# Aggregation of a graph attention layer as seven products of quarters, on numerators normalized in front of it

## The chip, the cores and the metric

The kernel runs on one core of one Trainium2 chip. The metric is device microseconds of one execution; lower is better. Engines are named as in the profile: PE is TensorE's matmul, PEld its weight load, DVE is VectorE, ACT is ScalarE, POOL is GpSimd, SP is SyncE, whose queue issues the DMAs.

## The reference

Two layers follow each other on `x` of 64 graphs with 256 nodes and 512 features in float32; one adjacency matrix `adj` (256 x 256) holds for all graphs. Layer 0 is a graph attention whose weights come from a sum of two logits of the nodes, layer 1 an attention with 8 heads. Cut to what matters:

```python
# layer 0
h = jnp.maximum(_layernorm(x, axis=-1), 0.0)
Wh = jnp.einsum('bnd,de->bne', h, W)
e_src = jnp.einsum('bnd,d->bn', Wh, a_src)
e_dst = jnp.einsum('bnd,d->bn', Wh, a_dst)
logits = e_src[:, :, None] + e_dst[:, None, :]
logits = jnp.where(logits >= 0, logits, 0.2 * logits)
logits = jnp.where(mask, -jnp.inf, logits)          # mask = adj == 0
attn = jax.nn.softmax(logits, axis=-1)
x = x + jnp.einsum('bnm,bmd->bnd', attn, Wh)
# layer 1
h = jnp.maximum(_layernorm(x, axis=-1), 0.0)
q, k, v = (split_heads(h @ Wn.T + bn) for n in 'qkv')
attn = softmax(where(mask, -inf, q k^T / 8))
x = x + (attn v, heads joined) @ Wo.T + bo
```

## The kernel before, in words

A group is one graph: two tiles of 128 nodes by 512 features. There are G = 64 groups. The stages of a group are Python generators; each step of one writes a few instructions. An order that is written out by hand (`first_half` and `second_half`, one entry for each step, with a number that says how many groups ahead of the loop's group the step works) interleaves the steps of up to six groups. One pass through the two lists is a cycle of the steady state. Within an engine, instructions run in the order written; across engines they are tied by semaphores.

TensorE's products in a cycle, by letter: O is the output projection of layer 1 (two groups back), K the projection to q and k, V to v, W layer 0's transform by `W`, U0 and US layer 0's aggregation, X1 the transposition of the normalized rows for layer 1, E0 the weights of layer 0, A the attention's scores, masks and products with v. O, W, V and K are each written as **seven products of quarters**: a product of a 2 x 2 block matrix with another takes seven block products instead of eight if sums of blocks are formed first and sums of products afterwards. `combine` (L163) forms four sums of quarters of the left side on GpSimd, `combine_w` those of the weights once at the start, `products` (L170) writes the seven products, each into its own bank of PSUM, and `add_up` (L189, the adds L192 to L203) adds the products on VectorE. For product 0 ScalarE copies instead (L762 for v).

A product in float32 gives two records in the trace for each matmul instruction, each with its weight load.

Layer 0 in a group:

- `normalize0` (N0, D0): ScalarE forms means and squares (L457, L463), GpSimd the inverse deviations (L474 to L476), ScalarE h (L504), VectorE four sums of products with two weight rows (L511), which are the nodes' logits `es` and `ed`; the unused product goes into the scratch tile `junk`.
- `weights0` (E0, three steps): TensorE transposes `es` into `pe` (L525); ScalarE takes two exponentials (L532, L533) into `e1` and `e2`. Then VectorE takes their maximum (L537), and GpSimd multiplies with the mask (`em`, L540) and adds the two tiles (`esum`, L542). Last, TensorE sums over nodes (`ps`, L556) and VectorE takes the reciprocal (`rb`, L558, L559).
- `aggregate0` (U0 twice, then US): `pu` = the numerators `em` times `h`, transposed, as 8 matmul instructions with 256 columns in two banks (L572); VectorE multiplies each bank with the reciprocals into `uT` (L579). In US `combine` forms the sums `us` for the transform.
- `transform0` (W): seven products with `W`, added to the rows of x (L643).

In layer 1, `normalize1` (N1) writes `xn` (L671), `transpose1` (X1) transposes it (`pt`, L692) and writes `hT` (L693), then `combine` forms `hs`. `scale` (AS) multiplies the heads' results `aT` with the reciprocals of their sums (L878), which SP's queue has spread by eight DMAs into `rb` of the attention; `combine` then forms `as`. `bias_rows` (BO) adds the bias to the rows on GpSimd (L871). `attention` masks the exponentials (L793), adds them (L795), and takes the reciprocals of the sums (L828).

All banks of PSUM (8) are one pool; a product takes the bank that came free first, so it waits for the reader of an earlier product:

```python
def bank(shape, name):
    return ps_mm.tile(shape, F32, tag="mm", name=name)
```

Around U0 the written order of a cycle is `... V, V, V, A, N0, N1, U0, V, AS, U0, X1, V, X1, V, X1` and then, in the next pass, `(load), O, D0, K, AS_OLD, O, K, O, E0, K, E0, ...`. So VectorE has, in this order: the adds of V, a mask of A, the multiplication of the first U0, the adds of V, the scaling of aT, the multiplication of the second U0, two adds of V, the add of O, the four L511. ScalarE has h, xn and then hT.

Of the kernel before, what the change touches and what calls it, by code (L numbers as in the profile page):

```python
# [9 lines left out]
F32 = mybir.dt.float32  # L10
I32 = mybir.dt.int32
AF = mybir.ActivationFunctionType
ALU = mybir.AluOpType
# [3 lines left out]
P = 128  # L17
# [7 lines left out]
END = object()  # L25
# [3 lines left out]
def kernel(  # L29
# [26 lines left out]
    nc = tc.nc  # L56
    B, N, D = x.shape
    NC = N // P
    DC = D // P
# [4 lines left out]
    HD = D // 2  # L64
# [67 lines left out]
    def bounded():  # L132
# [9 lines left out]
        B11, B21, B22, T1, T2, T3, T4N = range(7)  # L142
# [115 lines left out]
        def node_weights():  # L258

            wa_c = weights.tile([P, 2, DC], F32, tag="wa_c", name="wa_c")  # L260
            a_rows = [bank([P, D], f"pa_{j}") for j in range(2)]
            for j in range(2):
                nc.tensor.matmul(a_rows[j], ones[0:1, :], a_in[:, j, :], start=True, stop=True)
            pas = [bank([P, D], f"pwa_{j}") for j in range(2)]
            for c in range(DC):
                if c == DC // 2:
                    busy(4)
                for j in range(2):
                    junk = work.tile([P, D], F32, tag="junk", name=f"junk_a_{j}_{c}")
                    nc.vector.scalar_tensor_tensor(  # L270
                        junk, a_rows[j], 1.0, w_c[c // 2][:, c % 2, :], op0=ALU.mult, op1=ALU.mult,
                        accum_out=wa_c[:, j, c : c + 1],
                    )
                    nc.tensor.transpose(
                        pas[j][:, c * P : (c + 1) * P], wa_c[:, j, c : c + 1].to_broadcast([P, P]),
                        ident,
                    )
                    if c >= DC // 2:
                        busy(2)
            return pas  # L280
# [36 lines left out]

        def output_bias():

            terms = work.tile([P, 2, HD], F32, tag="junk", name="terms")  # L320
            for c in range(DC):

                rows = wo_sb[:, B11 : T3 + 1 : T3 - B11] if c < 2 else wo_sb[:, B21 : B22 + 1]
                part, bv_c = rows[:, :, c % 2, :], cols["bv"][:, c : c + 1]
                if c == 0:
                    nc.vector.tensor_scalar(terms, part, bv_c, None, op0=ALU.mult)
                else:
                    nc.vector.scalar_tensor_tensor(
                        terms, part, bv_c, terms, op0=ALU.mult, op1=ALU.add
                    )  # L330
            yield
            pb = bank([P, D], "pbias")
            nc.tensor.matmul(pb, ones, terms.rearrange("p j e -> p (j e)"), start=True, stop=True)
            nc.vector.tensor_add(bo_b, pb, bo_b)
            yield
# [23 lines left out]
        def constants():  # L359
# [46 lines left out]
                yield  # L406
            sq = weights.tile([P, 4], F32, tag="sq", name="sq")
            for j, col in enumerate((cols["bq"], cols["bk"])):
                junk = work.tile([P, DC], F32, tag="junk", name=f"junk_c_{j}")
                nc.vector.scalar_tensor_tensor(  # L410
                    junk, col, 1.0, col, op0=ALU.mult, op1=ALU.mult, accum_out=sq[:, j : j + 1]
                )
# [7 lines left out]
            )  # L420
            yield
            for j in range(2):
                junk = work.tile([P, D], F32, tag="junk", name=f"junk_w_{j}")
                nc.vector.scalar_tensor_tensor(
                    junk, wa[j], 1.0, wa[j], op0=ALU.mult, op1=ALU.mult, accum_out=sq[:, 2 + j : 3 + j]
                )
                yield
# [53 lines left out]
        def normalize0(g):  # L481

            xt = xts[g]
            h = big.tile([P, NT, D], F32, tag="h", name=f"h_{g}", bufs=2)
            es = small.tile([P, NT], F32, tag="es", name=f"es_{g}")
            ed = small.tile([P, NT], F32, tag="ed", name=f"ed_{g}")
            if g == 1:

                mv, rstd = norm_stats(xt, f"0_{g}", small)
                nmr = small.tile([P, NT], F32, tag="nmr", name=f"nmr0_{g}")  # L490
                nc.gpsimd.tensor_scalar(nmr, mv[:, :, 0], -1.0, 0.0, op0=ALU.mult, op1=ALU.add)
                nc.gpsimd.tensor_tensor(nmr, nmr, rstd, op=ALU.mult)
                yield
            else:
                stats = Stats(xt, h, f"0_{g}")
                for t in range(NT):
                    stats.mean(t)
                yield
                for t in range(NT):
                    stats.squares(t)  # L500
                nmr, rstd = stats.close()
                yield
            for t in range(NT):
                nc.scalar.activation(  # L504
                    h[:, t, :], xt[:, t, :], AF.Relu, bias=nmr[:, t : t + 1], scale=rstd[:, t : t + 1]
                )
            yield
            for t in range(NT):
                for dst, a in ((es, 0), (ed, 1)):
                    junk = work.tile([P, D], F32, tag="junk", name=f"junk_{g}_{t}")  # L510
                    nc.vector.scalar_tensor_tensor(  # L511
                        junk, (wa if g else pas)[a], 1.0, h[:, t, :], op0=ALU.mult, op1=ALU.mult,
                        accum_out=dst[:, t : t + 1],
                    )
            nodes[g] = h, es, ed
            yield

        def weights0(g):
# [41 lines left out]
            edges[g].append(rs)  # L560
            yield

        def aggregate0(g):

            h = nodes.pop(g)[0]
            em = edges[g][0]
            uT = big.tile([P, DC, TOK], F32, tag="uT", name=f"uT_{g}")
            for dp in range(0, DC, 2):
                pu = bank([P, 2, N], f"pu_{g}_{dp}")
                for d in range(2):  # L570
                    for m in range(NC):
                        nc.tensor.matmul(  # L572
                            pu[:, d, :],
                            h[:, m, (dp + d) * P : (dp + d + 1) * P],
                            em[:, m, :],
                            start=(m == 0),
                            stop=(m == NC - 1),
                        )
                nc.vector.tensor_mul(  # L579
                    uT[:, dp : dp + 2, :], pu, edges[g][1].unsqueeze(1).to_broadcast([P, 2, N])  # L580
                )
                yield

            def a(t, j):
                return uT[:, 2 * j : 2 * j + 2, t * P : (t + 1) * P]

            del edges[g]
            sums0[g] = a, four_sums("us", g)
            combine(a, sums0[g][1])
            yield  # L590
# [366 lines left out]
        def aside(n=1):  # L957
            for _ in range(n):
                next(side, END)

        K, V, W, O = (project_qk, 0), (project_v, 0), (transform0, 1), (output, -2)
        N0, D0, E0, U0 = (normalize0, 3), (normalize0, 2), (weights0, 2), (aggregate0, 2)
        US, N1, X1 = (aggregate0, 1), (normalize1, 1), (transpose1, 1)
        A, A_OLD, BO = (attention, 0), (attention, -1), (bias_rows, 0)
        AS, AS_OLD = (scale, -1), (scale, -2)
        first_half = [
            (load, 3), O, D0, K, AS_OLD, O, K, O, E0, K, E0, O, K, O, US, A_OLD, K, O, K, BO, O, K, E0,
        ]
        second_half = [
            A_OLD, A, A, W, N0, W, W, V, N0, W, W, W, N1, W, N1, A, V, V, V, A, N0, N1, U0, V, AS,  # L970
            U0, X1, V, X1, V, X1,
        ]

# [23 lines left out]
        for i in range(G + 1):  # L997
            if i == G - 2:
                load_wo()
            todo = first_half + second_half  # L1000
            if i == 0:
                todo = first + [A, A, W, N0, E0] + second_half[5:19] + second_half[20:]
            elif i >= G - 1:
                todo = end if i == G else last
            for n, (stage, ahead) in enumerate(todo):
                if i == 0 and n in (5, 10):
                    next(bias)
                if i == 0 and n == 12:
                    combine_w(wv_sb)
                if i == 0 and n == len(first) + 1:  # L1010
                    combine_w(wq_sb)
                    prepare_biases()
                if i == 0 and n == len(first) + 18:
                    combine_w(wk_sb)
                if i == 1 and n == 4:
                    step(attention, 0)
                if i == 1 and n == 9:
                    combine_w(wo_sb)
                if i == 1 and n == 13:
                    step(bias_rows, 0)  # L1020
                step(stage, i + ahead)
                if i and n % 4 == 1:
                    aside()
# [209 lines left out]
```

## Time and profile before

| what | value |
|---|---|
| median of 3 runs | 2868.86 us (2867.56 to 2870.16) |
| the profiled execution | 2867.64 us, of which the span of the instructions is 2865.9 us |
| granted TensorE clock | 1.0 |
| busy: PE, DVE, ACT, POOL | 2848.8, 2343.6, 1235.0, 1214.5 us |
| a cycle of the steady state (one group) | 44.08 us |
| aggregation pu<-em,h (L572) | 1008 records, 238.1 us busy |
| multiplication uT<-pu,rb (L579) | 126 instructions, 682 ns mean |
| GpSimd's sums of quarters (L165 to L168) | 733 to 1162 ns each, by what runs beside them |

A line of a timeline reads: start in us from the span's start, length in us, engine, line of the kernel, operation, written tile <- read tiles, shape, number of instructions merged; in brackets, idle time of that engine before it and what ended it. Where several are merged, the length goes from the first start to the last end, and the ends of matmuls are modelled, so paces are read from starts.

### The profile page before, as it was taken

Reading aid. Unit: us, or ns where it says so; the run is one execution under the profiler, and the core shown is the slowest. Engines: PE = TensorE matmul, PEld = TensorE weight load, DVE = VectorE, ACT = ScalarE, POOL = GpSimd, SP = SyncE. Lnnn points to the kernel's source line nnn. Section 1 sums busy time; section 2 is a strip of 40 time slices with the busy share of each in tenths; the row PEclk is TensorE's granted clock in tenths of the full one; section 3 lists DMA queues with packets and bytes.
Section 4 is the critical chain, followed back from the end, with each engine's and each line's share of the span. In section 5 each row is a group of like instructions: output and inputs, shape, how many; then the busy total and the mean of one; then the engine's idle time right before and its main releaser. Section 6 shows DMA issues by size and latency. Waiting matters only on the chain. (4 is left out here: it accounts for less than half of the span.)

```text
span 2865.9 us, 50571 instructions
## 1 busy us (share of the span) xinstructions
PE 2848.8 (99%) x19584; PEld 2461.1 (86%) x19584; DVE 2343.6 (82%) x3641; ACT 1235.0 (43%) x2984; POOL 1214.5 (42%) x1406
## 2 busy tenths in 40 slices
PE   9999999999999999999999999999999999999998
PEld 6888888888888888888888888888888888888886
DVE  7888888888888888888888888888888888888875
ACT  5444444443543444435434444354344443443432
POOL 3444534435445344354453443544534435445331
PEclk9999999999999999999999999999999999999999
DMA  4122122221221222212212222122122221221221
GB/s 133 23 38 38 34 41 33 36 45 31 38 38 34 41 33 35 45 31 38 38 33 41 33 35 45 30 38 39 32 41 33 36 45 31 38 40 32 34 41 28
DMA packets 82810, 110.82 MB, mean 39 GB/s; under 512 B 11524, under 2 KB 48644, under 8 KB 82566
## 3 DMA queue, kind: packets, MB, share of 16 engines
q1 hardware_dynamic: 82470, 107.53, 23.5%
q8 instruction: 157, 2.57, 0.3%
q14 instruction: 87, 0.71, 0.1%
q0 software_dynamic: 96, 0.01, 0.0%
HBM read 41.43 MB, written 33.55 MB: 26 GB/s over the span
## 5 line engine op out<-in xcount | busy, mean ns | idle before, releaser
L643 DVE TENSOR_TENSOR x<-po,x 128x1024 f32<-128x1024 f32 x875 | 594.4, 686 | 209.9 <-PE po L207 203.0
L474 POOL TENSOR_SCALAR ve<-ssq 128x2 f32<-128x2 f32 x127 | 25.0, 197 | 1072.3 <-ACT h L463 827.7
L793 DVE TENSOR_TENSOR ex<-ex,maskT 128x512 f32<-128x512 f32 x512 | 361.1, 747 | 0.0
L788 ACT ACTIVATE ex<-psc 128x512 f32<-128x512 f32 x512 | 257.7, 627 | 90.2 <-PE psc L780 90.2
L813 ACT COPY aT<-pav 128x512 f32<-128x512 f32 x128 | 74.9, 585 | 498.5 <-PE pav L805 467.4
L216 PEld LDWEIGHTS pqk<-hs,wq_sb 128*128 128x128 f32 x2016 | 264.4, 192 | 12.9
L216 PE MATMUL pqk<-hs,wk_sb 128*128 128x128 f32 x2016 | 266.3, 275 | 0.0
L216 PE MATMUL pqk<-hs,wq_sb 128*128 128x128 f32 x2016 | 265.8, 275 | 0.0
L511 DVE SCALAR_TENSOR_TENSOR junk<-wa,h 128x512 f32<-128x512 f32 x252 | 255.1, 1012 | 12.5 <-ACT h L504 1.1
L207 PE MATMUL pv<-wv_sb,hs 128*128 128x256 f32 x1024 | 262.8, 379 | 0.6 <-DVE v L194 0.5
L207 PE MATMUL po<-wo_sb,as 128*128 128x256 f32 x992 | 255.2, 380 | 0.0
L207 PE MATMUL po<-w_sb,us 128*128 128x256 f32 x1008 | 248.5, 379 | 0.0
L216 PEld LDWEIGHTS pqk<-hs,wk_sb 128*128 128x128 f32 x2016 | 245.4, 192 | 0.0
L780 PE MATMUL psc<-qk 64*128 64x256 f32 x2048 | 239.0, 383 | 1.0 <-DVE rc L828 1.0
L572 PE MATMUL pu<-em,h 128*128 128x256 f32 x1008 | 238.1, 379 | 0.0
L805 PE MATMUL pav<-ex,v 128*64 128x256 f32 x2048 | 235.4, 382 | 0.0
L780 PEld LDWEIGHTS psc<-qk 64*128 64x128 f32 x2048 | 193.1, 187 | 47.6 <-issue 25.0
L740 ACT ACTIVATE p<-pqk,bias 128x128 f32<-128x128 f32 x252 | 71.8, 367 | 346.5 <-PE pqk L216 346.5
L828 DVE RECIPROCAL rc<-psm 128x256 f32<-128x256 f32 x64 | 112.4, 1756 | 133.0 <-PE psm L820 133.0
L871 POOL TENSOR_TENSOR x<-x,bo_b 128x512 f32<-128x512 f32 x128 | 218.2, 1723 | 0.0
L805 PEld LDWEIGHTS pav<-ex,v 128*64 128x64 f32 x2048 | 141.4, 137 | 85.6 <-DVE x L643 19.9
L207 PEld LDWEIGHTS po<-w_sb,us 128*128 128x128 f32 x1008 | 191.4, 190 | 26.2 <-DVE x L643 0.2
(188 smaller groups left out, 5880.9 us busy)
## 6 DMA issues: line engine op xcount, KB each, us to landing
x<-in_x_dram SPq DMA_DIRECT2D x64, 512.0 KB, 5.6
out_dram<-x SPq DMA_DIRECT2D x128, 256.0 KB, 2.0
rb<-rc SPq DMA_DIRECT2D x496, 64.0 KB, 4.9
wq_sb<-in_L_gnn_Wq_dram SPq DMA_DIRECT2D x4, 256.0 KB, 8.5
wk_sb<-in_L_gnn_Wk_dram SPq DMA_DIRECT2D x4, 256.0 KB, 6.6
w_sb<-in_L_gnn_W_dram SPq DMA_DIRECT2D x4, 256.0 KB, 6.6
wv_sb<-in_L_gnn_Wv_dram SPq DMA_DIRECT2D x4, 256.0 KB, 6.6
wo_sb<-in_L_gnn_Wo_dram SPq DMA_DIRECT2D x4, 256.0 KB, 6.0
```

The costliest lines, as they stand in the source:

```text
L207: nc.tensor.matmul(dst[:, 0:HD], left[:, c, :], wt[:, slot, c, :], start=c == 0, stop=c == 1)
L216: nc.tensor.matmul(dst[:, at : at + P], wt[:, slot, c, e * P : (e + 1) * P], left[:, c, :], start=c == 0, stop=c == 1,)
L511: nc.vector.scalar_tensor_tensor(junk, (wa if g else pas)[a], 1.0, h[:, t, :], op0=ALU.mult, op1=ALU.mult, accum_out=dst[:, t : t + 1],)
L572: nc.tensor.matmul(pu[:, d, :], h[:, m, (dp + d) * P : (dp + d + 1) * P], em[:, m, :], start=(m == 0), stop=(m == NC - 1),)
L643: nc.vector.tensor_add(dst, src, dst)
L780: nc.tensor.matmul(psc[r][:, m, :], qk[rows, 2 + e % 2, m * P : (m + 1) * P], qk[rows, e % 2, :], start=True, stop=True,)
L788: nc.scalar.activation(ex[:, r, :, :], psc[r], AF.Exp, scale=SCALE)
L793: nc.vector.tensor_mul(ex[:, r, :, :], ex[:, r, :, :], maskT)
L805: nc.tensor.matmul(pav[r * DH : (r + 1) * DH, i, :], v[j][:, m, at : at + DH], pair[i][:, r, m, :], start=(m == 0), stop=(m == NC - 1),)
L813: nc.scalar.copy(aT[j], pav)
L828: nc.vector.reciprocal(rc, psm)
L871: nc.gpsimd.tensor_tensor(part, part, bo_b, op=ALU.add)
```

## The change

For groups 3 to 63 the aggregation is written as seven products of quarters, like the projections. A new stage `quarters0` (Q0), one step early in the second half, forms on GpSimd the four sums of quarters of `h` (`hq`), multiplies the numerators `em` in place with the reciprocals (two instructions), and forms four differences of quarters of `em` (`eq`). `aggregate0` then writes seven products, each two matmul instructions of 128 columns into a bank of its own, four in its first step and three in its second; ScalarE copies product 0 into `uT`, VectorE adds up the others with seven adds. The multiplication with the reciprocals behind the products is gone. Groups 1 and 2 keep the old form (group 0 has its own path).

Two steps of E0 move in the written order: the one with the transpositions and exponentials is now behind the third K of the cycle instead of the second, the one with the maximum and the mask behind the fourth K instead of the third.

To make room in SBUF, the scratch tiles `junk` use the buffer of `e2`, and `terms` that of `rb`. New lines of the kernel after are 58 higher from `aggregate0`'s end on.

```diff
-                    junk = work.tile([P, D], F32, tag="junk", name=f"junk_{g}_{t}")
+                    junk = work.tile([P, D], F32, tag="e2", name=f"junk_{g}_{t}")
...
+        PLAIN = 3
+
+        def quarters0(g):
+
+            if g >= PLAIN:
+                h = nodes[g][0]
+                em, rb = edges[g]
+
+                def a(i, k):
+                    return h[:, k, i * HD : (i + 1) * HD]
+
+                s = big.tile([P, 4, HD], F32, tag="hq", name=f"hq_{g}")
+                combine(a, s)
+                for m in range(NC):
+                    nc.gpsimd.tensor_tensor(em[:, m, :], em[:, m, :], rb, op=ALU.mult)
+
+                def quarter(k, j):
+                    return em[:, k, j * P : (j + 1) * P]
+
+                t = work.tile([P, 4, P], F32, tag="eq", name=f"eq_{g}")
+                for to, x, y in (
+                    (0, quarter(0, 1), quarter(0, 0)), (1, quarter(1, 1), t[:, 0]),
+                    (2, quarter(1, 1), quarter(0, 1)), (3, quarter(1, 0), t[:, 1]),
+                ):
+                    nc.gpsimd.tensor_tensor(t[:, to], x, y, op=ALU.subtract)
+                right = {B11: quarter(0, 0), B21: quarter(1, 0), B22: quarter(1, 1)}
+                for to, slot in enumerate((T1, T2, T3, T4N)):
+                    right[slot] = t[:, to]
+                nodes[g] = h, (a, s, right)
+            yield
+
         def aggregate0(g):
 
-            h = nodes.pop(g)[0]
+            h, parts = nodes.pop(g)[0:2]
             em = edges[g][0]
             uT = big.tile([P, DC, TOK], F32, tag="uT", name=f"uT_{g}")
-            for dp in range(0, DC, 2):
+            if g >= PLAIN:
+                left, s, right = parts
+                s2 = work.tile([P, 4, P], F32, tag="s2", name=f"s2u_{g}")
+
+                def product(dst, left, slot):
+                    for e in range(2):
+                        nc.tensor.matmul(
+                            dst[:, e * P : (e + 1) * P], left[:, e * P : (e + 1) * P], right[slot],
+                            start=True, stop=True,
+                        )
+
+                def dst(i, j):
+                    return uT[:, 2 * i : 2 * i + 2, j * P : (j + 1) * P]
+
+                def read(n, ps):
+                    ps = ps[:, 0:HD].rearrange("p (e n) -> p e n", e=2)
+                    if n == 0:
+                        nc.scalar.copy(dst(0, 0), ps)
+                    add_up(n, ps, dst, s2[:, 0:2, :])
+
+                step_of = products(left, s, f"pu_{g}", product, read)
+                for n in range(7):
+                    next(step_of)
+                    if n in (3, 6):
+                        yield
+                assert next(step_of, END) is END
+            for dp in range(0, DC, 2) if g < PLAIN else ():
...
+        Q0 = (quarters0, 2)
...
         first_half = [
-            (load, 3), O, D0, K, AS_OLD, O, K, O, E0, K, E0, O, K, O, US, A_OLD, K, O, K, BO, O, K, E0,
+            (load, 3), O, D0, K, AS_OLD, O, K, O, K, E0, O, K, E0, O, US, A_OLD, K, O, K, BO, O, K, E0,
         ]
         second_half = [
-            A_OLD, A, A, W, N0, W, W, V, N0, W, W, W, N1, W, N1, A, V, V, V, A, N0, N1, U0, V, AS,
+            A_OLD, A, Q0, A, W, N0, W, W, V, N0, W, W, W, N1, W, N1, A, V, V, V, A, N0, N1, U0, V, AS,
             U0, X1, V, X1, V, X1,
         ]
```

More of the change, by code (lines that the diff above doesn't have):

```diff
@@ L268, in node_weights @@
                 for j in range(2):
-                    junk = work.tile([P, D], F32, tag="junk", name=f"junk_a_{j}_{c}")
+                    junk = work.tile([P, D], F32, tag="e2", name=f"junk_a_{j}_{c}")
                     nc.vector.scalar_tensor_tensor(
@@ L318, in output_bias @@
         def output_bias():
-            terms = work.tile([P, 2, HD], F32, tag="junk", name="terms")
+            terms = work.tile([P, 2, HD], F32, tag="rb", name="terms")
             for c in range(DC):
@@ L408, in constants @@
             for j, col in enumerate((cols["bq"], cols["bk"])):
-                junk = work.tile([P, DC], F32, tag="junk", name=f"junk_c_{j}")
+                junk = work.tile([P, DC], F32, tag="e2", name=f"junk_c_{j}")
                 nc.vector.scalar_tensor_tensor(
@@ L422, in constants @@
             for j in range(2):
-                junk = work.tile([P, D], F32, tag="junk", name=f"junk_w_{j}")
+                junk = work.tile([P, D], F32, tag="e2", name=f"junk_w_{j}")
                 nc.vector.scalar_tensor_tensor(
@@ L1001, in bounded @@
             if i == 0:
-                todo = first + [A, A, W, N0, E0] + second_half[5:19] + second_half[20:]
+                todo = first + [A, A, W, N0, E0] + second_half[6:20] + second_half[21:]
             elif i >= G - 1:
```

## The prediction

> **What bounds the kernel now.** I read the busy shares first, then one steady cycle in a window, then the timeline of TensorE, and last the waits. The busy shares (engine, busy us, share of the span, instructions):
>
> ```profile
> PE 2848.8 (99%) x19584; PEld 2461.1 (86%) x19584; DVE 2343.6 (82%) x3641; ACT 1235.0 (43%) x2984; POOL 1214.5 (42%) x1406
> ```
>
> TensorE is busy for the whole span, but ends of matmuls are modelled, so a share of 99% alone proves little. The timeline tells it by the starts. The aggregations of one group begin at 1390.08 us, those of the next at 1434.16 us: a cycle is 44.08 us. In the window of that cycle (length, busy us of PE, PEld, DVE, ACT, POOL) all other engines have room:
>
> ```profile
> 1390.08:1434.16 44.08, 44.08 (x305) 38.40 (x304) 36.44 (x57) 19.09 (x47) 19.26 (x22) 1.00 0.24 37
> ```
>
> The TensorE timeline around the change (start, length, engine, line, tiles, count):
>
> ```profile
> 1390.08 1.89 PE L572 MATMUL pu<-em,h 128*128 128x256 f32 x8
> 1391.81 1.03 PE L207 MATMUL pv<-wv_sb,hs 128*128 128x256 f32 x4
> 1392.67 1.89 PE L572 MATMUL pu<-em,h 128*128 128x256 f32 x8
> 1394.40 0.60 PE L692 MATMUL pt<-ident,xn 128*128 128x128 f32 x4
> 1394.84 1.03 PE L207 MATMUL pv<-wv_sb,hT 128*128 128x256 f32 x4
> 1395.70 0.60 PE L692 MATMUL pt<-ident,xn 128*128 128x128 f32 x4
> 1396.14 1.03 PE L207 MATMUL pv<-wv_sb,hs 128*128 128x256 f32 x4
> 1397.01 1.03 PE L207 MATMUL po<-wo_sb,aT 128*128 128x256 f32 x4
> 1397.87 1.05 PE L216 MATMUL pqk<-hT,wq_sb 128*128 128x128 f32 x8
> 1398.76 1.06 PE L216 MATMUL pqk<-hT,wk_sb 128*128 128x128 f32 x8
> ```
>
> The reader is to see that each start is the start before it plus the records' own pace: nothing waits. A record of 256 columns goes by 0.216 us (1.73 us for 8), one of 128 columns by 0.111 us (0.89 us for 8). So the time is the sum of TensorE's records, and a change pays if it takes records away and lets nothing make TensorE wait. The list of waits agrees: VectorE, ScalarE and GpSimd wait for TensorE, and TensorE's own waits are small.
>
> **What the Trainium skill says.** "TensorE: Matmul & The Clock Gate", section "Wait — 56ns, not 53.3ns?", has a small fixed cost for each matmul beside its columns. The trace agrees in kind: two records of 128 columns take 0.222 us, one of 256 takes 0.216. "SBUF — State Buffer", section "Who interferes with whom", says that a VectorE instruction with two SBUF inputs contends with a GpSimd instruction that reads SBUF. The trace agrees: the add at L199, beside GpSimd's adds of the bias, takes 1710 ns, its twin at L198 692. "VectorE: DVE Perf Modes", section "The DRAIN you can't avoid", lets no VectorE instruction start before the one ahead has emptied the pipe, with a semaphore costing nothing more. The trace differs: adds of 0.41 us start 0.33 apart when independent, 0.51 apart when the second needs the first (L192 to L194, 1389.97 to 1390.48). I take the trace.
>
> **The change part by part.** 61 of the 64 groups get it (groups 3 to 63).
>
> TensorE. Removed for a group: 8 products of 256 columns, 16 records, 16 x 0.216 = 3.46 us. Added: 7 products of two matmuls of 128 columns, 28 records. No row shows them; the nearest is L216, same shape and a weight load for each, 0.111 us: 28 x 0.111 = 3.11 us. Lower bound: the pace of the transpositions, 0.109 (0.44 us for 4), 3.05 us; upper: busy time by record with the pipeline's tail, 266.3 / 2016 = 0.132, 3.70 us. I take 0.111. Gain 0.34 us of a group, 61 x 0.34 = 20.7 us.
>
> VectorE. Removed: two multiplications at L579, 0.68 us each. Added: seven adds of 128x256 out of PSUM at 0.41 us, as for v at L192 to L203. Busy +1.5 us, 37.9 of 43.74 us: not the bound, but late in one place. ScalarE: one copy of 128x256 more, 0.37 us as at L762. It stands behind the normalization of xn (L671):
>
> ```profile
> 1390.22 1.50 ACT L504 ACTIVATE h<-x,nmr,rstd 128x512 f32<-128x512 f32 x2
> 1391.92 1.52 ACT L671 ACTIVATE xn<-x,nmr,rstd 128x512 f32<-128x512 f32 x2 [0.20 <-POOL nmr L476]
> ```
>
> That is the critical place; I follow it in the clock of this cycle. TensorE would be done with products 0 to 3 at 1391.86, a product of v at 1392.73, products 4 to 6 at 1394.06, and then go on 0.34 us earlier than in the timeline above: first transposition 1394.06, v 1394.50, second transposition 1395.36, v 1395.80, output product 1396.67. Weight loads want their data 0.1 to 0.2 us before. ScalarE's copy of product 0 runs from 1393.35 to 1393.72; its bank is the one that the first transposition takes: slack 0.2. VectorE's first add needs the copy: 1393.77 to 1394.18; its bank goes to the v product of 1394.50: slack 0.2. Second add 1394.28 (it needs the first: 0.51), third 1394.62, the two adds of the v product at 1394.95 and 1395.28, the scaling of aT (L878, 0.68) 1395.62 to 1396.30. The output product needs it at 1396.67, its weights at about 1396.45: slack 0.15, the narrowest. So I cost these waits at nothing, covered by the 3.5 us of matmuls that TensorE has between product 0 and the first of these takers, and the 2.6 us after it; if the chain is late by more than the slack, TensorE waits for the excess.
>
> Behind that VectorE still has the second scaling, four adds and two of v: the output product's add starts at 1398.84 instead of 1398.07, and the four L511 end at 1404.26 instead of 1403.49. The transpositions of the logits (pe, L525, at 1403.17) read these: at 1402.83 they would wait 0.3 us for the third. Moved one product of q and k (1.78 us) later, at 1404.6, they have 1.5 us of slack. What moves with them: four exponentials, the maximum on VectorE (L537, 1405.98, now about 1408.2, behind two adds), then GpSimd's queue: em (1406.74, now 1408.9), esum, four sums of us, two adds of the bias, all some 2 us later. First takers: ps at 1415.43 needs esum (ready by 1411.4), the transform's second product at 1425.2 needs us (by 1415.5). Hidden. No DMA is issued by what moves; SP's queue keeps its order.
>
> GpSimd. Added for a group: four sums of quarters of h and two multiplications of 128x256, 0.73 us alone and 1.17 beside VectorE (L165, L168), and four subtractions of 128x128: from 0.73 at 256 and 1.27 at 512 elements I work out 0.46, at most 0.7. Sum 6.2 to 9.8 us. They stand after the bias adds, from about 1418.8, in an idle stretch of 13.74 us (before L474 at 1430.19), and end between 1425.0 and 1428.6; the products take them at 1433.8. What they can hurt is VectorE's masks at 1422.72 (L793 twice, L795): in contention 1.81 + 1.10 us instead of 1.28 + 0.69, so 0.94 more, and VectorE waits 1.01 us for TensorE right there. Covered, by 0.07 us; beyond it the first adds of the transform come later, and they have 0.84 us of waiting behind them. Shared scratch tiles (junk into e2, terms into rb) and the start, end and groups 0 to 2: nothing.
>
> Sum: 2867.64 (the profiled execution: span 2865.9 and 1.7 around it) - 20.7 = 2846.9; the median of the runs shown is 1.2 above that execution, so 2848.2.
>
> **The rivals.**
> 1. *The chain behind ScalarE's copy is a bit late.* Each 0.1 us beyond the 0.15 of slack costs 6.1 us over 61 groups. Against it: cycles repeat to 0.01 us, so no chance delays. For it: my slack is about as large as the errors in my starts. 0.05 to 0.25 us of waiting: 2851 to 2863.
> 2. *Slower: VectorE's added adds do not overlap.* Each of the five adds ahead of the scaling is followed only after 0.51 us: the scaling starts at 1393.77 + 5 x 0.51 = 1396.32 and ends at 1397.00, 0.55 after the output product's weights want it. Net 0.55 - 0.34 = 0.21 us lost, 61 x 0.21 = 12.8 us: 2882. It decides from 0.49 us of lateness on. For it: the writes are strided and each reads what another wrote; against it: the v adds overlap at 0.33.
> 3. *Short records cost their busy time.* 28 x 0.132 = 3.70 against 238.1 / 1008 = 0.236, 16 x 0.236 = 3.78: gain 0.08 us, 5 us in all, 2864, no change that shows. Against it: starts, not busy times, add up to the cycle.
>
> **How the numbers follow.** Full gain 0.62 (2848), rival 1 0.18, rival 3 0.08, rival 2 0.12. A measurement tells 0.2% (5.7 us) from no change. Faster 0.62 + 0.18 = 0.80, same 0.08, slower 0.12. Best case: records at 0.109, 61 x 0.41 = 25 us: 2844. The range goes from there to 2861, nearly all of rival 1; rivals 2 and 3, together 0.20, lie outside.
>
> **What would show it.** Right: a cycle of 43.74 us; records of the seven products 0.111 apart; transpositions 0.34 us nearer to the aggregation's start, with no idle time of the weight loads before them or before the first output product; logits' transpositions without a wait; GpSimd's ten instructions done before L474. Wrong: idle time of TensorE laid to the copy of product 0, to its adds, or to the scaling of aT; or starts of the short records 0.12 us apart or more.

## The result, and the profile after

The changed kernel takes 2847.49 us (median of 4 runs, 2846.97 to 2848.37); the kernel before, beside it, 2868.21 us. The ratio is 0.9927, interval 0.9915 to 0.9940: 0.73% faster. The forecast was 2848.2 us, in a range of 2844 to 2861. The profiled execution took 2846.97 us, its span is 2845.2 us, 20.7 us less than before; the sum had forecast 20.7 us less.

Busy shares of the kernel after:

```profile
PE 2828.9 (99%) x20316; PEld 2472.3 (87%) x20316; DVE 2473.5 (87%) x3946; ACT 1257.3 (44%) x3045; POOL 1607.0 (56%) x2016
```

One cycle of it, from the start of an aggregation to the next (length, busy us of PE, PEld, DVE, ACT, POOL, then the granted clock, the DMA share and GB/s):

```profile
1467.50:1511.25 43.75, 43.75 (x318) 38.58 (x317) 38.59 (x62) 19.47 (x48) 25.64 (x32) 1.00 0.24 37
```

TensorE is still busy for the whole cycle, and the cycle is 0.33 us shorter (44.08 before). VectorE went from 36.44 to 38.59 us, GpSimd from 19.26 to 25.64, in a shorter cycle. TensorE's timeline of the same place as before:

```profile
1467.50 0.61 PE L606 MATMUL pu<-em,h 128*128 128x128 f32 x4
1467.94 0.61 PE L606 MATMUL pu<-eq,hq 128*128 128x128 f32 x4
1468.39 0.61 PE L606 MATMUL pu<-em,h 128*128 128x128 f32 x4
1468.84 0.61 PE L606 MATMUL pu<-eq,hq 128*128 128x128 f32 x4
1469.28 1.03 PE L207 MATMUL pv<-wv_sb,hs 128*128 128x256 f32 x4
1470.15 0.61 PE L606 MATMUL pu<-eq,hq 128*128 128x128 f32 x4
1470.59 0.61 PE L606 MATMUL pu<-eq,h 128*128 128x128 f32 x4
1471.04 0.61 PE L606 MATMUL pu<-em,hq 128*128 128x128 f32 x4
1471.49 0.60 PE L750 MATMUL pt<-ident,xn 128*128 128x128 f32 x4
...
1474.09 1.03 PE L207 MATMUL po<-wo_sb,aT 128*128 128x256 f32 x4
1474.95 1.05 PE L216 MATMUL pqk<-hT,wq_sb 128*128 128x128 f32 x8
```

Four records of a product take 0.445 us, 0.111 each, the pace of the q and k products; the first transposition comes 3.99 us after the start of the aggregation instead of 4.32. No line has idle time before it. Nor have the weight loads of the first transposition and of the first output product, where the prediction looked for a sign of being wrong:

```profile
1471.38 0.47 PEld L750 LDWEIGHTS pt<-ident,xn 128*128 128x128 f32 x4
...
1473.88 0.84 PEld L207 LDWEIGHTS po<-wo_sb,aT 128*128 128x128 f32 x4
```

The chain that the prediction called critical, on ScalarE and on VectorE:

```profile
1469.34 1.52 ACT L729 ACTIVATE xn<-x,nmr,rstd 128x512 f32<-128x512 f32 x2 [0.20 <-POOL nmr L476]
1470.77 0.35 ACT L617 COPY uT<-pu 128x256 f32<-128x256 f32 x1
```

```profile
1471.15 0.42 DVE L192 TENSOR_TENSOR s2u<-uT,pu 128x256 f32<-128x256 f32 x1 [0.57 <-ACT uT L617]
1471.70 0.42 DVE L194 TENSOR_TENSOR uT<-uT,pu 128x256 f32<-128x256 f32 x1
1472.04 0.41 DVE L196 TENSOR_TENSOR uT<-s2u,pu 128x256 f32<-128x256 f32 x1
1472.37 0.41 DVE L198 TENSOR_TENSOR v<-v,pv 128x256 f32<-128x256 f32 x1
1472.70 0.41 DVE L199 TENSOR_TENSOR v<-s2v,pv 128x256 f32<-128x256 f32 x1
1473.03 1.29 DVE L936 TENSOR_TENSOR aT<-aT,rb 128x512 f32<-128x512 f32 x2
```

The first add starts 3.65 us after the aggregation (predicted 3.69), the scaling of aT 5.53 us (predicted 5.54). The new wait, VectorE for ScalarE's copy, is there (0.57 us in brackets), but VectorE is not the bound. GpSimd's added work:

```profile
1493.45 2.50 POOL L929 TENSOR_TENSOR x<-x,bo_b 128x512 f32<-128x512 f32 x2
1495.91 0.73 POOL L165 TENSOR_TENSOR hq<-h 128x256 f32<-128x256 f32 x1
...
1500.14 0.90 POOL L588 TENSOR_TENSOR eq<-em 128x128 f32<-128x128 f32 x1
...
1502.73 0.45 POOL L588 TENSOR_TENSOR eq<-em,eq 128x128 f32<-128x128 f32 x1
1507.28 0.19 POOL L474 TENSOR_SCALAR ve<-ssq 128x2 f32<-128x2 f32 x1 [4.09 <-ACT h L463]
```

It lasts 7.3 us, from 1495.91 to 1503.18, and 4.09 us of idle time are left before the inverse deviations: the stretch of 13.74 us before the change has taken it.

### The profile page after: what moved, and what is told of

It reads as the page before. It is cut to its first block, busy times and chain, and to the rows that moved or that the text cites. A ratio compares the mean times of both kernels' runs of the same rounds, so it can differ in the third digit from the quotient of the medians.

```text
span 2845.2 us, 53317 instructions
## 1 busy us (share of the span) xinstructions
PE 2828.9 (99%) x20316; PEld 2472.3 (87%) x20316; DVE 2473.5 (87%) x3946; ACT 1257.3 (44%) x3045; POOL 1607.0 (56%) x2016
## 5 line engine op out<-in xcount | busy, mean ns | idle before, releaser
L851 DVE TENSOR_TENSOR ex<-ex,maskT 128x512 f32<-128x512 f32 x512 | 435.3, 890 | 0.0
L511 DVE SCALAR_TENSOR_TENSOR junk<-wa,h 128x512 f32<-128x512 f32 x252 | 276.6, 1098 | 7.9 <-ACT h L504 1.1
L540 POOL TENSOR_TENSOR em<-e,maskT 128x512 f32<-128x512 f32 x62 | 79.6, 1283 | 321.7 <-DVE e L537 312.0
L165 POOL TENSOR_TENSOR hs<-hT 128x256 f32<-128x256 f32 x64 | 47.0, 735 | 319.2 <-PE pv L207 319.2
L853 DVE TENSOR_TENSOR sm<-ex 128x512 f32<-128x512 f32 x256 | 210.5, 822 | 8.9
L216 PEld LDWEIGHTS pqk<-hT,wq_sb 128*128 128x128 f32 x1512 | 198.2, 192 | 9.6
```

The lines of the kernel that those rows point to most:

```text
L165: nc.gpsimd.tensor_tensor(s[:, 0], a(1, 0), a(1, 1), op=ALU.add)
L216: nc.tensor.matmul(dst[:, at : at + P], wt[:, slot, c, e * P : (e + 1) * P], left[:, c, :], start=c == 0, stop=c == 1,)
L511: nc.vector.scalar_tensor_tensor(junk, (wa if g else pas)[a], 1.0, h[:, t, :], op0=ALU.mult, op1=ALU.mult, accum_out=dst[:, t : t + 1],)
L540: engine.tensor_tensor(em, e1, maskT, op=ALU.mult)
L851: nc.vector.tensor_mul(ex[:, r, :, :], ex[:, r, :, :], maskT)
L853: nc.vector.tensor_add(sm, ex[:, :, 0, :], ex[:, :, 1, :])
```

## The experiments

The theory: TensorE's records set the time, 0.33 us less a cycle in 61 cycles, and all else is hidden, in two places narrowly: the chain behind ScalarE's copy, and the logits' transpositions, which need E0's move. Each kernel below is the changed kernel with one edit. The kernel before took 2868.37 us beside the first four and 2868.53 us beside the last four. Cycles are distances of aggregation starts in the trace, 43.75 us without an edit.

**The steps of E0 back in their old places.**

```diff
-            (load, 3), O, D0, K, AS_OLD, O, K, O, K, E0, O, K, E0, O, US, A_OLD, K, O, K, BO, O, K, E0,
+            (load, 3), O, D0, K, AS_OLD, O, K, O, E0, K, E0, O, K, O, US, A_OLD, K, O, K, BO, O, K, E0,
```

> Seven products kept, the two steps of E0 back in their old places (transpositions of the logits behind the second K). My theory: the third L511 now ends 13.3 us after the start of the aggregation, and the second transposition would start at about 12.9 us, so TensorE waits 0.4 to 0.65 us in each of 61 cycles: cycle 44.15 to 44.4 us, 2872 to 2887 us, more than the gain of the products. Rival (the move was not needed, the wait is hidden): cycle 43.75 us, 2847.5 us. A named wait of PE for DVE junk L511 tells them apart.

Measured: 2881.45 us, 1.0046 of before (1.0029 to 1.0063), cycle 44.32 us. TensorE's timeline of that kernel shows the wait:

```profile
1454.21 0.27 PE L525 MATMUL pe<-ident,es 128*128 128x128 f32 x1
1454.84 0.32 PE L525 MATMUL pe<-ident,es 128*128 128x128 f32 x1 [0.36 <-DVE junk L511]
1455.00 1.06 PE L216 MATMUL pqk<-hT,wq_sb 128*128 128x128 f32 x8
```

The second transposition starts 0.63 us after the first instead of 0.11, and the next product follows after 0.16 us instead of 0.11. So without the move the seven products are slower than the old form: the wait of 0.57 us a cycle is more than the 0.33 gained.

**The old aggregation in all groups, with the new order.**

```diff
-        PLAIN = 3
+        PLAIN = G
```

> All groups keep the old aggregation, only E0's steps stand later. My theory: the move alone is worth nothing, the cycle is 44.08 us as before, 2868 us, since TensorE has the same records and waited for nothing in the old order. Rival (part of the gain comes from the move, through less contention of GpSimd with VectorE): a cycle of less than 44.0 us, below 2863 us.

Measured: 2868.0 us, 0.9998 of before (0.9989 to 1.0006), cycle 44.08 us. The move alone is worth nothing; it is a condition of the gain. This kernel also shares the scratch tiles as the changed one does, so the gain doesn't come from that either.

**Product 6 issued twice.**

```diff
-                    for e in range(2):
+                    for e in (0, 1, 0, 1) if slot == B22 else range(2):
```

> The two matmuls of product 6 are issued twice (same values written again): 32 records of 128 columns in place of 28, as eight products of quarters would have. My theory: TensorE is the bound and a short record costs its pace, 4 x 0.1115 = 0.446 us more, cycle 44.19 us, 61 x 0.446 = 27.2 us, 2874.7 us, slower than the old form with its 16 records of 256 columns. Rival (short records cost their busy time, 0.132 us): 61 x 0.528 = 32.2 us, 2879.7 us. Rival (TensorE has hidden room): 2847.5 us.

Measured: 2874.88 us, 1.0024 of before (1.0015 to 1.0033), cycle 44.19 us. In TensorE's timeline of that kernel the eight records stand 0.111 apart (0.89 us to the next line), and no wait is added:

```profile
1440.15 1.06 PE L606 MATMUL pu<-em,hq 128*128 128x128 f32 x8
1441.04 0.60 PE L750 MATMUL pt<-ident,xn 128*128 128x128 f32 x4
```

The cycle grows by 0.447 us, four times the pace, and not by 0.528, four times the busy time. This excludes hidden room on TensorE. The kernel has as many records as eight products of quarters would have, and it is slower than the old form with its 16 records of 256 columns: the gain is the eighth product that isn't there, less the cost of short records.

**The add of product 3 written twice.**

```diff
                     add_up(n, ps, dst, s2[:, 0:2, :])
+                    if n == 3:
+                        add_up(n, ps, dst, s2[:, 0:2, :])
```

> VectorE's add of product 3 is written twice (same values again), one add of 0.33 us more in the chain from ScalarE's copy to the scaling of aT. In the trace of the kernel after, that scaling ends 0.16 us before the weights of the output product are loaded. My theory: the slack is 0.1 to 0.15 us, TensorE waits for the rest, 0.2 us in each of 61 cycles: cycle 43.95 us, 2859 us, with a wait for DVE aT before the output product. Rival (the chain is far from the critical one, or TensorE's queue takes it up): cycle 43.75 us, 2847.5 us.

Measured: 2860.77 us, 0.9975 of before (0.9964 to 0.9985), cycle 43.98 us. Its list of waits has a line that the kernel after has not:

```profile
PEld po L207 <- DVE aT L938: 21.9, 60, 0.4
```

**Half of that add written once more.**

```diff
+                    if n == 3:
+                        nc.vector.tensor_add(dst(1, 0)[:, 0, :], s2[:, 0, :], ps[:, 0, :])
```

> After the add of product 3, half of it (128 of 256 elements) is added once more (same values). From add_twice: 0.331 us more in the chain cost 0.22 us of a cycle, so the slack is 0.11 us. A half add should lengthen the chain by about 0.20 us (from 0.33 us at 256 and 0.60 at 512 elements). My theory (a threshold: only the excess over the slack is paid): 0.09 us of a cycle, 5.5 us, 2853 us. Rival (each add in the chain is paid in proportion, no slack): 0.13 us of a cycle, 2855.5 us or more; rival (free up to a larger slack): 2847.5 us.

Measured: 2853.43 us, 0.9948 of before (0.9932 to 0.9965), cycle 43.85 us. The time is the expected one partly by luck: both lengths that I had used, 0.33 and 0.20 us, were 0.13 too short, and the slack too small, which cancels. The traces give the lengthening itself, from the first add to the scaling of aT: 1.88 us after, 2.34 with the whole add (0.46 more), 2.21 with half of it (0.33 more). The cycle pays 0.24 and 0.10. Both leave the same slack, 0.22 to 0.23 us: it is a threshold, and only the excess is paid. VectorE's, the weight load's and TensorE's timelines of the kernel with half an add, whose aggregation starts at 1471.18:

```profile
1475.71 0.42 DVE L196 TENSOR_TENSOR uT<-s2u,pu 128x256 f32<-128x256 f32 x1
1476.16 0.29 DVE L620 TENSOR_TENSOR uT<-s2u,pu 128x128 f32<-128x128 f32 x1
...
1477.77 0.73 PEld L207 LDWEIGHTS po<-wo_sb,aT 128*128 128x128 f32 x4 [0.24 <-DVE aT L938]
...
1477.77 1.13 PE L207 MATMUL po<-wo_sb,aT 128*128 128x256 f32 x4
1478.73 1.05 PE L216 MATMUL pqk<-hT,wq_sb 128*128 128x128 f32 x8
```

The weight load of the output product starts late, 6.59 us after the aggregation instead of 6.38, but the product's first record stands where it stood, at 6.59. What the cycle pays is in the four records: 0.96 us to the next line instead of 0.86.

**The same double add, with product 0 copied by VectorE.**

```diff
-                        nc.scalar.copy(dst(0, 0), ps)
+                        nc.vector.tensor_copy(dst(0, 0), ps)
...
+                    if n == 3:
+                        add_up(n, ps, dst, s2[:, 0:2, :])
```

> As add_twice, but product 0 is copied by VectorE instead of ScalarE, so the chain no longer starts behind the normalization of xn on ScalarE. My theory (the chain's start is ScalarE's copy): VectorE can copy at 2.98 us after the start of the aggregation, 0.41 us long, the first add then starts near 3.50 instead of 3.65, so 0.10 to 0.15 us of add_twice's 0.22 us of waiting a cycle go: 2852 to 2855 us. Rival (the chain's start is VectorE's own queue, and its additional copy only lengthens it): add_twice or more, 2861 to 2880 us.

Measured: 2853.8 us, 0.9948 of before (0.9931 to 0.9964), cycle 43.82 us; three cycles take 44.18, for a reason that stays open. VectorE's timeline of that kernel, whose aggregation starts at 1472.28:

```profile
1475.27 0.42 DVE L617 COPY uT<-pu 128x256 f32<-128x256 f32 x1
1475.79 0.42 DVE L192 TENSOR_TENSOR s2u<-uT,pu 128x256 f32<-128x256 f32 x1
...
1478.10 1.28 DVE L938 TENSOR_TENSOR aT<-aT,rb 128x512 f32<-128x512 f32 x2
```

The first add starts after 3.51 us instead of 3.65, and 7.0 of the 13.3 us that the double add cost are gone, although VectorE has an instruction more. The scaling starts at 5.82 us, 0.29 later than after the change, and the cycle pays 0.07: the same slack a third time. So the chain begins at ScalarE's copy, behind xn, as the prediction had it.

**GpSimd's sums of quarters of h twice, and four times.**

```diff
                 combine(a, s)
+                combine(a, s)
```

The other kernel has that line four times in all.

> GpSimd forms the four sums of quarters of h twice (same values), 2.9 us more in a cycle. In the trace of the kernel after GpSimd idles 4.1 us after its added work, before the inverse deviations (L474). My theory: hidden, the cycle stays 43.75 us, 2847.5 us. Rival (GpSimd's reads slow VectorE's masks beside them, which then hold up the transform's adds and the statistics behind): 0.1 us or more of a cycle, above 2853 us.

Measured: 2851.08 us, 0.9940 of before (0.9924 to 0.9957): between the theory and the rival. The steady cycle is 43.75 us, so the theory holds there. The median is 3.6 us longer than that of the changed kernel. In the profiled execution the first two cycles with the new form take 46.51 and 44.39 us instead of 43.97 and 44.06, which makes 2.9 us; the rest is within the spread of the runs (2849.73 to 2852.31). A wait of the weight load of the transpositions for the copy of product 0, up to 2.4 us, appears twice in this trace. My expectation left the start out.

> GpSimd forms the four sums of quarters of h four times (same values), 8.6 us more in a cycle, 4.5 us more than the idle stretch before L474. My theory: the differences of quarters of em end 44.3 us after the aggregation's start instead of 35.7, behind the second product that reads them at 44.2, and the inverse deviations of both normalizations come 2 us or more late for ScalarE, which then delays xn, the copy of product 0 and the chain behind it: TensorE waits 1 to 3 us in each of 61 cycles, 2908 to 3030 us. Rival (GpSimd has room elsewhere in the cycle, since 25.6 + 8.6 = 34.2 of 43.7 us busy): 2847.5 us.

Measured: 3100.05 us, 1.0802 of before (1.0784 to 1.0821), cycles of 47.1 to 50.0 us. The waits of that kernel:

```profile
ACT h L504 <- POOL nmr L476: 233.8, 62, 9.3
PEld pt L751 <- ACT uT L618: 151.2, 61, 3.3
PE pt L751 <- ACT uT L618: 139.6, 61, 3.1
PEld pu L607 <- POOL eq L589: 43.0, 60, 0.7
```

The mechanism is the expected one, GpSimd's late deviations hold ScalarE, whose copy holds the transposition; the size is above what I had. The mean granted clock of that execution is also lower (0.983), and the trace tells the two apart. Of the 58 steady cycles (without the first four), 33 take 47.1 to 47.2 us: in one of them (from 1555.71) TensorE loses 0.7 us before the second product and 2.5 before the first transposition, and some 0.2 in the first records behind these waits. The other 25 take 48.6 to 50.0 us, with a stretch at half the clock from about the end of the second wait on. In the cycle from 1937.39 (TensorE's timeline, then the busy shares of a window, with 0.50 for the granted clock):

```profile
1944.62 1.12 PE L751 MATMUL pt<-ident,xn 128*128 128x128 f32 x4 [2.31 <-ACT uT L618]
1945.53 1.92 PE L207 MATMUL pv<-wv_sb,hT 128*128 128x256 f32 x4
1947.24 0.96 PE L751 MATMUL pt<-ident,xn 128*128 128x128 f32 x4
```

```profile
1944.60:1946.00 1.40, 1.38 (x6) 1.29 (x7) 1.27 (x4) 0.00 (x0) 0.00 (x0) 0.50 0.00 0
```

Four records of v take 1.71 us there instead of 0.87. The half clock thus costs about 1.5 us in 24 of those 25 cycles (the longest also waits longer); the waits cost over 3 us in every cycle. GpSimd's stretch is a margin, not free room: 2.9 us more cost the steady cycle nothing; 8.6 us more cost 3.4 us a cycle even at the full clock, where up to 3 was expected.

## Why the prediction was right, point by point

- *TensorE's pace.* 0.111 us for a short record, measured 0.111; the cycle came out at 43.75 us, predicted 43.74. That the total agrees to 0.1 us is partly luck: the steady cycles gained 0.33 us, not 0.34, which makes 20.2 us in 61 of them, and the other 0.5 comes from the first cycles and the end, which the sum put at nothing. The choice of the pace read from starts over the busy time per record is what the doubled product confirms; rival 3 is out.
- *The chain behind ScalarE's copy.* Start and end are right to 0.04 us. The slack was put at 0.15 us and is 0.22 to 0.23. It was counted to the normal start of the weight load; but the first half of the scaling, 0.68 us long, ends 0.38 us before the output product's first record, and since 0.22 of it can be used up, its data may come after that start, up to an estimated 0.16 us before the record. Rival 1 had the right place, with nothing to pay there.
- *Rival 2, the adds that don't overlap.* The adds start 0.33 us apart in the trace, except for the second, 0.55 after the first that it needs (0.51 was taken). The rival's place is real, and lateness there is paid beyond the slack, as the double add shows; its premise is not.
- *The logits' transpositions.* Right that they must move; the wait without the move was put at 0.3 us and is 0.57. The mis-sized term is the four L511: they were shifted with their lengths of before (the first 0.88 us), but the first now runs beside GpSimd's sums as the others do and takes 1.19 us; the mean went from 1012 to 1098 ns. The slack after the move is 1.2 us, not 1.5 (the third ends at 1480.82, the place is at 1482.04).
- *GpSimd.* 7.3 us, in the 6.2 to 9.8 predicted; the start came 0.3 us before the predicted one, the end lies in the predicted stretch. The subtractions take 0.79 to 0.90 us beside the masks and 0.45 alone; 0.46 to 0.7 was predicted, so this term was too small beside VectorE. The others, at 0.73 us each, stayed at the low end, and the sum in its range.
- *VectorE beside GpSimd.* The first masks and their add lengthened by 0.65 us (0.94 predicted), and VectorE's wait for TensorE there fell from 1.01 to 0.35 us: covered. But GpSimd's later queue now meets other masks too; L793 (L851 after) went from 747 to 890 ns on average. VectorE's cycle is 38.59 us instead of the 37.9 that the sum had. The twin at L198, which the prediction set against L199 as the undisturbed one, also has an add of the bias beside it in that cycle (it starts at 1412.97, the add of the bias at 1413.00): overlap alone does not set the length.

## What to carry to other kernels

When an engine's records fill the span, cost a change of their number or shape with the distance of starts of the same shape, not with busy time; splitting records has a price of its own (0.222 against 0.216 us here), so it pays only if whole products vanish. Then follow the data out of the new instructions to the next instruction that wants it or its buffer, in the order written: what counts is the first taker, and its slack is a threshold. An order tuned for the old chain may have to move with it, and the move alone shows nothing.

## What the runs showed of the hardware that I had not expected

An add of VectorE that overwrites the result of the add before it starts 0.45 us later (L196 and L620 of the kernel with half an add), an independent one 0.33 us later; so doubling an add that had added 0.33 us to the chain cost it 0.46 us.

A wait of TensorE can cost more than its length. In the kernel with GpSimd's sums four times, the trace's record of the granted clock shows 29 stretches at 0.50, in which records take twice as long. Their starts lie whole multiples of 3.413 us apart, to 0.002 us (367.594, 463.167 and 606.527 us: 28 and 42 of them), and all but the one at the end last one or two of these steps. In 57 steady cycles TensorE waits equally long, about 2.5 us, before the first transposition. In the 24 of them with such a stretch the wait ends between 0.34 us before and 0.34 us after a point of this grid; in the 33 without, 0.36 to 1.12 us after one. So in this kernel it is the place of the wait on the grid that parts the cycles in which the clock drops from the others.

And the order alone moves the contention of VectorE and GpSimd. In the kernel with the old aggregation and the new order, the adds at L199 took 1203 ns instead of 1710 and the bias adds on GpSimd 1280 instead of 1723, while the masks went from 747 to 829 ns; with the seven products the masks went on to 890, and L511 from 1013 to 1098. None of this reached TensorE: the cycle with the order alone stayed at 44.08 us.
